# Attention scores computed twice, the second time with keys on partitions, in units of 8 heads

## The chip, the cores and the metric

The kernel runs on one core of a Trainium2 chip. Its engines are TensorE (PE, with its weight loads shown as PEld), VectorE (DVE), ScalarE (ACT), GpSimd (POOL) and SyncE (SP), which issues the DMAs. The metric is the device time of one execution in microseconds (us). Each engine works through its own queue in order; an instruction that waits holds back all that is queued behind it on that engine.

## The reference, cut to what matters

Four layers run one after the other on x of shape (4, 256, 512): attention with an adapter, a clustered feed-forward, a state-space mixer and the feed-forward again. The change lies in the first.

```python
q, k, v = split(einsum('btc,oc->bto', layernorm(x), w_attn))   # 32 heads of 16
q, k = rope(q), rope(k)
scores = einsum('bhqd,bhkd->bhqk', q, k) / sqrt(16)
attn = softmax(where(causal, scores, -inf), axis=-1)
y = einsum('bhqk,bhkd->bhqd', attn, v)
ascores = gating * softmax(einsum('bhqd,hkd->bhqk', q, ak) / sqrt(512))  # 10 adapter keys
y = y + einsum('bhqk,hkd->bhqd', ascores, av)
x = x + einsum('btc,oc->bto', y, w_proj)
```

## The kernel before

The attention stage goes through 4 batches of 256 tokens. `prepared(b)` normalises two token tiles of 128, turns them, makes queries, keys and values with three products each (operands in a high and a low part, `mm3`, L107) and applies the rotary embedding (`rotated`, L274: three DVE operations and one of POOL, L281 to L287). It is a generator: the next batch's steps are taken one by one between the units of the batch at hand.

`pieces(b, q)` (L371) takes 8 heads. `stacked` lays down high and low parts of each head as four slots of 16 (ACT L305, POOL L306), the fourth slot zero; PE turns them (tile trp, L380), and DVE copies the queries and ACT the keys out (L382). The result has 64 partitions for each head, two heads above one another, so that one product of 64 terms gives a head's scores.

A unit `u` has 4 heads, so there are 32 units. `scores(b, u)` (L413) works with queries on partitions. For each half c of the queries and each of two row positions pr (partitions 0 to 63 or 64 to 127) it fills one PSUM bank with two heads' scores over all 256 keys (L425, two products on the same 64 rows), adds the causal mask with a product of the identity and a table of -1e30 (L429), takes the row maximum on DVE (L434) and makes the exponentials on ACT, one head at a time, with the row sum as a by-product (L437). `turn` (L443) turns the exponentials on PE, 12 transposes of 128x128 for a unit (tile ptr, L452), and DVE and ACT copy them to SBUF (L453). `weigh` (L456) multiplies them with the values, four heads side by side on 32 columns each (L462 and L468), and ACT copies the product (L473). `gathered` (L476) turns it back (L479) and divides by the row sums (L484, L485).

`adapter_scores`, `adapted`, `closed` and `ended` make the adapter's part, add it, turn y (L530) and project it (tile po). In the last batch the tiles of the feed-forward that follows (tile pd, `Feed.tile`, L196) run between the units.

The main loop (L608) is a software pipeline: scores of unit i, transposes of unit i-1, weighing of unit i-2, gathering of unit i-3, then the next pieces, then one step of each waiting job. This is the order of the program text; a scheduler then reorders instructions within each engine's queue. PSUM has 8 banks: 2 for everything tagged "m", 3 for scores, 2 for transposed exponentials, 1 for the weighted values.

Of the kernel before, what the change touches and what calls it, by code (L numbers as in the profile page):

```python
# [35 lines left out]
# Columns of the constant table.  # L36
# [12 lines left out]
def constants():  # L49
    """Masks, selections and rotary tables: they depend on the shapes alone."""  # L50
# [18 lines left out]
    # [token, token tile, queries or keys, cos or sin, term]  # L69
# [8 lines left out]
def hybrid_kernel(  # L78
# [23 lines left out]
    def split(hl, v, engine=nc.vector):  # L102
        """v as the sum of two parts that each fit the products' 12 bits."""
        nc.scalar.copy(hl[0], v)  # L104
        engine.tensor_tensor(hl[1], v, hl[0].bitcast(F32), ALU.subtract)  # L105

    def mm3(o, ls, rs, first=True, last=True):  # L107
        """o = the sum over k of ls[k].T @ rs[k], operands in two parts."""
# [7 lines left out]
    def warmed(o, vs):  # L116
        """Products whose result nobody reads: they keep the array's clock up in a wait."""
        for v in vs:
            nc.tensor.matmul(o[:, : v.shape[1]], ones, v, start=True, stop=True)

    def primed(func):
        """Has the scalar engine load a function's table ahead of its use."""
# [3 lines left out]
    class Norm:  # L126
        """A layer's normalisation of x."""
# [32 lines left out]
        def turn(self, xn, tr, xs):  # L160
            """In two parts, features on partitions."""
# [4 lines left out]
        def turned(self, t, xn, tr, xs):  # L166
            """A token tile normalised, in two parts, features on partitions."""
# [4 lines left out]
    class Feed:  # L172
        """One clustered layer, a token tile at a time."""
# [22 lines left out]
        def tile(self, t, xs, halves):  # L196
            """What a token tile becomes where its columns are selected, and its hits."""
# [22 lines left out]
        def select(self, cnt, rows):  # L220
            """The columns of the clusters that any token hits, as a mask."""
# [10 lines left out]
    def attention(later):  # L232
        with ExitStack() as es:
# [6 lines left out]
            ps = pool("a_m", 2, space=PSUM)  # L240
            ps_s = pool("a_s", 3, space=PSUM)
            ps_t = pool("a_t", 2, space=PSUM)
# [31 lines left out]
            def rotated(pq, c, f, name):  # L274
                """Rotary embedding, tokens on partitions; f: 0 for queries, 1 for keys."""
# [14 lines left out]
            # Parts of 8 heads side by side so that one product of 48 terms carries  # L290
            # high * high + high * low + low * high.
            NS = 2
            stacks = [[w1.tile([P, 8, 4, HD], F32R, name=f"st{f}{i}") for i in range(NS)] for f in range(2)]
            for f in range(2):
# [6 lines left out]
            def stacked(src, f, n=P):  # L301
                st = stacks[f][turn_at[f] % NS]
                turn_at[f] += 1
# [7 lines left out]
            # Adapter keys and values, spread to block diagonals.  # L311
# [7 lines left out]
            def adapter_weights():  # L319
# [9 lines left out]
                for q in range(4):  # L329
                    s = stacked(ak[:20, q * 8 : q * 8 + 8, :], 1, 20)  # L330
# [3 lines left out]
                    # The heads' columns: two more to the right in each of the four products.  # L334
# [16 lines left out]
            vs = [w1.tile([P, 2, C + HD], F32, name=f"av{i}") for i in range(2)]  # L351
            for v in vs:
                nc.gpsimd.memset(v[:, :, C:], 0.0)
# [3 lines left out]
            def prepared(b):  # L357
                """Steps that make a batch's queries, keys and values."""
# [8 lines left out]
                for c in range(2):  # L367
                    nc.scalar.copy(vs[b % 2][:, c, :C], projected(xs[c], wv_s, where))
                    yield

            def pieces(b, q):  # L371
                """Queries and keys of 8 heads, on partitions of (2 heads, 64 terms)."""
# [29 lines left out]
            state = {}  # L402

            def begin(b):
                state[b] = {
                    "as": p2.tile([P, 2, NH, NA], F32, name="as"),
                    "rs": p2.tile([P, 2, NH], F32, name="rs"),
# [5 lines left out]
            def scores(b, u):  # L413
                """Softmax numerators of 4 heads, rows on partitions."""
                qT, kT = turned_[b, u // 2]
# [788 lines left out]
```

## Time and profile before

| what | us |
|---|---|
| median of 3 runs | 1928.0 (1927.61 to 1932.41) |
| span of the profiled execution, first to last instruction | 1929.2 |
| first score product of a batch starts at | 37.3, 122.8, 204.8, 287.0 |
| last projection of the attention ends at | 387.9 |
| granted TensorE clock, mean of the span | 0.989 |

The span lies within the range of the three runs, 1.2 us above their median. So the profiled execution can stand for them. Columns of the views: a row of a group has line, engine, operation, output and inputs, shapes and count, then the busy time in us and the mean ns of one, then the idle time of the engine before them and what ended it. A row of the time order has the start in us, the duration in us, engine and line; "x2" means that two were merged. Durations of PE's products overlap, because each starts while the one before still drains. What a product costs PE is therefore read from start to start.

### The profile page before, as it was taken

The numbers are of one execution on the slowest core, as the hardware profiler recorded it, in microseconds if no ns is written. First come the engines' busy times: TensorE is split into PE (matmuls) and PEld (weight loads), VectorE is DVE, ScalarE is ACT, GpSimd is POOL, SyncE is SP. The second block draws the span as 40 slices with busy tenths as digits, with TensorE's granted clock in tenths as the row PEclk, the third lists the DMA queues.
The fourth block names the chain that finished last, engine by engine and source line by source line (L and its number), as shares of the span: only waits on it lengthen the run. The fifth ranks groups of instructions, "written<-read, shape, count | busy, mean of one in ns | idle before, by whom it ended". The sixth has DMA issues, their size and how long they took to land.

```text
span 1929.2 us, 29952 instructions
## 1 busy us (share of the span) xinstructions
PE 1882.0 (98%) x10690; PEld 1470.6 (76%) x10690; DVE 1478.0 (77%) x2324; ACT 1383.7 (72%) x2873; POOL 346.0 (18%) x306
## 2 busy tenths in 40 slices
PE   7999999989999999999999999999999999999997
PEld 6767767767777777877787777777777777787786
DVE  5556557679998878877877797778777877877777
ACT  5665667557898677876877787778677877786753
POOL 4112120011231111122121111211111111121100
PEclk7999999989999999999999999999999999999999
DMA  4000000014555554555454455445444545455341
GB/s 140 1 1 1 1 22 24 12 38 153 166 193 182 158 166 146 154 153 164 152 164 149 154 164 160 149 144 181 148 164 151 160 157 159 133 169 158 117 126 48
DMA packets 151909, 240.35 MB, mean 125 GB/s; under 512 B 12368, under 2 KB 77520, under 8 KB 151760
## 3 DMA queue, kind: packets, MB, share of 16 engines
q1 hardware_dynamic: 151760, 238.44, 39.0%
q8 instruction: 84, 1.38, 0.3%
q14 instruction: 65, 0.53, 0.1%
HBM read 202.75 MB, written 35.65 MB: 124 GB/s over the span
## 4 chain that ended last, share of the span: by engine, by line
PE 83%; DVE 5%; ACT 5%; DMA 2%; issue 2%; SPq 0%; DVEq 0%; ACTq 0%
PE pp L112 12%; PE pp L114 12%; PE pp L113 11%; PE pyy L923 8%; PE pog L112 6%; PE pog L114 6%; PE pog L113 6%; PE sc L425 3%; PE trx L908 3%; PE ptr L452 2%; PE py L462 1%; DMA wor<-in_wout_dram 1%; PE sc L429 1%; PE trp L380 1%; DVE acc L849 1%
## 5 line engine op out<-in xcount | busy, mean ns | idle before, releaser
L112 PE MATMUL pp<-mx,w 128*128 128x512 f32 (+1 forms) x1160 | 469.1, 404 | 7.2 <-DVE acc L849 6.7
L114 PE MATMUL pp<-mx,w 128*128 128x512 f32 (+1 forms) x1160 | 459.0, 396 | 0.0
L113 PE MATMUL pp<-mx,w 128*128 128x512 f32 (+1 forms) x1160 | 458.1, 395 | 0.0
L849 DVE SCALAR_TENSOR_TENSOR acc<-pp,cw_s,acc 128x1012 f32<-128x1012 f32 (+2 forms) x240 | 304.8, 1270 | 23.7 <-ACT acc L842 23.1
L897 DVE TENSOR_TENSOR em<-em,gm 128x1536 f32<-128x1536 f32 x128 | 228.3, 1784 | 88.9 <-ACT em L891 80.6
L112 PEld LDWEIGHTS pp<-mx,w 128*128 128x128 f32 x1160 | 218.8, 189 | 68.3 <-issue 10.3
L114 PEld LDWEIGHTS pp<-mx,w 128*128 128x128 f32 x1160 | 218.6, 188 | 49.3 <-issue 0.4
L113 PEld LDWEIGHTS pp<-mx,w 128*128 128x128 f32 x1160 | 219.0, 189 | 45.1 <-issue 0.7
L946 POOL TENSOR_TENSOR sq<-sq,acc 128x1024 f32<-128x1024 f32 x55 | 132.6, 2411 | 584.0 <-ACT acc L945 584.0
L885 POOL TENSOR_SCALAR_AFFINE_SELECT r<-r 128x512 f32<-128x512 f32 x128 | 128.8, 1007 | 550.1 <-DMA r<-cumd 427.4
L104 ACT CAST w<-wr 128x512 fp32r<-128x512 f32 x144 | 88.5, 615 | 193.2 <-PE pp L113 169.9
L112 PE MATMUL pog<-wo,gh 128*128 128x512 f32 x512 | 204.2, 399 | 0.0
L114 PE MATMUL pog<-wo,gh 128*128 128x512 f32 x512 | 200.4, 392 | 0.0
L113 PE MATMUL pog<-wo,gh 128*128 128x512 f32 x512 | 199.7, 390 | 0.0
L890 ACT ACTIVATE em<-r,col_t 128x128 f32<-128x128 f32 x512 | 164.9, 390 | 48.3 <-PE pyy L923 46.9
L923 PE MATMUL pyy<-em,xd 128*64 128x256 f32 (+1 forms) x2048 | 188.7, 329 | 2.0 <-DVE em L897 1.9
L923 PEld LDWEIGHTS pyy<-em,xd 128*64 128x64 f32 x2048 | 133.1, 137 | 64.8 <-issue 21.1
L893 ACT ACTIVATE em<-r,col_t 128x128 f32<-128x128 f32 x512 | 166.4, 388 | 0.0
L881 DVE TENSOR_SCALAR em<-r,col_t 128x128 f32<-128x128 f32 x512 | 136.6, 326 | 11.8 <-PE pyy L923 10.1
L909 DVE TENSOR_TENSOR xd<-trx,dt_t 128x512 f32<-128x512 f32 x128 | 86.2, 683 | 61.6 <-PE trx L908 61.4
L105 DVE TENSOR_TENSOR w<-wr,w 128x512 fp32r<-128x512 f32 x139 | 98.0, 706 | 43.1 <-ACT w L104 42.4
L437 ACT ACTIVATE e<-sc,nmx 128x128 f32<-128x128 f32 (+1 forms) x256 | 105.4, 425 | 14.9 <-DVE nmx L434 14.8
(285 smaller groups left out, 3320.7 us busy)
## 6 DMA issues: line engine op xcount, KB each, us to landing
wr<-in_win_dram SPq DMA_DIRECT2D x287, 256.0 KB, 2.9
r<-cumd SPq DMA_DIRECT2D x128, 512.0 KB, 4.2
spill<-gb SPq DMA_DIRECT2D x63, 512.0 KB, 2.9
gr<-spill SPq DMA_DIRECT2D x120, 256.0 KB, 3.5
wor<-in_wout_dram SPq DMA_DIRECT2D x64, 256.0 KB, 3.1
out_dram<-x SPq DMA_DIRECT2D x8, 256.0 KB, 2.3
x<-in_x_dram SPq DMA_DIRECT2D x1, 1536.0 KB, 9.9
gr<-spill SPq DMA_DIRECT2D x8, 192.0 KB, 2.6
```

Source lines behind the costliest of these rows:

```text
L112: nc.tensor.matmul(o, lh, rh, start=(first and k == 0), stop=False)
L113: nc.tensor.matmul(o, lh, rl, start=False, stop=False)
L114: nc.tensor.matmul(o, ll, rh, start=False, stop=(last and k == n - 1))
L437: nc.scalar.activation(es_[c][:, 2 * j + pr, :], sc[:, j, :n], AF.Exp, bias=nm[:, j : j + 1], accum_out=rs[:, c, h : h + 1],)
L849: nc.vector.scalar_tensor_tensor(av[:, :, d:], pv[:, :, : L - d], cw_s[:, ch, tap : tap + 1], av[:, :, d:], ALU.mult, ALU.add,)
L881: nc.vector.tensor_scalar(e[:, b, 2, :], rv[:, b, 1, :], col_t[:, h, b, 1:2], 0.0, ALU.subtract, ALU.min,)
L885: nc.gpsimd.affine_select(rv[:, :, 0, :], rv[:, :, 0, :], pattern=[[0, B], [1, P]], compare_op=ALU.is_ge, fill=-1e30, base=0, channel_mult ...
L890: nc.scalar.activation(e[:, b, 1, :], rv[:, b, 1, :], AF.Exp, bias=col_t[:, h, b, 2:3])
L893: nc.scalar.activation(e[:, b, 0, :], rv[:, b, 0, :], AF.Exp, bias=col_t[:, h, b, 0:1])
L897: nc.vector.tensor_tensor(e, e, gm, ALU.mult)
L923: nc.tensor.matmul(py[d, b, k * P :], xd[:, 2 * b + k, d], es2[hh][:, b, 2 * k : 2 if k == 0 else 3, :].rearrange("p s i -> p (s i)"), sta ...
L946: (nc.gpsimd if n < NB - 1 else nc.vector).tensor_tensor(sq, sq, x2, ALU.add)
```

## The change

The transposed exponentials go. Instead the scores are computed a second time with keys on partitions, so that the exponentials come out as `weigh` needs them. The row maximum, which is now needed along the free axis of the second product, is made a term of it: slot 3 of the keys, until now zero, holds a one in its first place, and the same row of the queries receives minus the maximum. A unit is now 8 heads, so there are 16 iterations of the loop instead of 32.

For each unit, `tops` computes the first scores with the products alternating between the two row positions, masks them, takes the maxima on DVE as before (six reductions of 128x512 instead of eight of two sizes), turns the maxima on PE, copies them on ACT, and two DMAs on SP write them into the queries' rows 48 and 112. `numerators` of the unit before computes the second scores and takes the exponentials, a whole bank at a time and without a row sum; POOL then sets the entries behind the causal line to zero (`affine_select`). The row sum comes from a column of ones beside each head's 16 values. PSUM is dealt out anew: 3 banks "m", 4 for both kinds of scores, 1 for the weighted values.

```diff
-            ps = pool("a_m", 2, space=PSUM)
-            ps_s = pool("a_s", 3, space=PSUM)
-            ps_t = pool("a_t", 2, space=PSUM)
+            ps = pool("a_m", 3, space=PSUM)
+            ps_s = pool("a_s", 4, space=PSUM)
             ps_y = pool("a_y", 1, space=PSUM)
...
+            VW = HD + 1
+            vs = [w1.tile([P, 2, NH * VW + HD], F32, name=f"av{i}") for i in range(2)]
             for v in vs:
-                nc.gpsimd.memset(v[:, :, C:], 0.0)
+                nc.gpsimd.memset(v, 1.0)
+            for v in stacks[1]:
+                nc.gpsimd.memset(v[:, :, 3, 0:1].bitcast(F32), 1.0)
...
+            def tops(b, q):
+                qT, kT = turned_[b, q]
+                nm = p2.tile([P, 2, NMW], F32, name="nmx", tag="nmx")
+                def banks(parts):
+                    made = []
+                    for c, js in parts:
+                        n = (c + 1) * P
+                        pair = [
+                            ps_s.tile([P, len(js), n], F32, name="sc", tag="sc") for _ in range(2)
+                        ]
+                        for i, j in enumerate(js):
+                            for pr in range(2):
+                                rows = slice(64 * pr, 64 * pr + 64)
+                                nc.tensor.matmul(
+                                    pair[pr][:, i, :], qT[rows, j, c * P : (c + 1) * P], kT[rows, j, :n],
+                                    start=(i == 0), stop=False,
+                                )
+                        made += [(c, js, pr, sc) for pr, sc in enumerate(pair)]
+                    for c, js, pr, sc in made:
+                        n = (c + 1) * P
+                        nc.tensor.matmul(
+                            sc[:, :, n - P :], identb, negb.unsqueeze(1).to_broadcast([P, len(js), P]),
+                            start=False, stop=True,
+                        )
+                        at = pr * 4 + js[0]
+                        nc.vector.tensor_reduce(
+                            nm[:, c, at : at + len(js)], sc, AX.X, ALU.max, negate=True
+                        )
+                banks([(1, (0, 1)), (1, (2, 3))])
+                yield
+                banks([(0, (0, 1, 2, 3))])
+                tr = ps.tile([NMW, 2, P], F32, name="trm", tag="m")
+                for c in range(2):
+                    nc.tensor.transpose(tr[:, c, :], nm[:, c, :], ident)
+                mT = p2.tile([8, 2, P], F32R, name="mT", tag="mT")
+                nc.scalar.copy(mT, tr[:8])
+                for pr in range(2):
+                    load(
+                        qT[64 * pr + 48 : 64 * pr + 49].bitcast(F32),
+                        mT[4 * pr : 4 * pr + 4].rearrange("p c i -> p (c i)").bitcast(F32),
+                    )
+                yield
...
+            def numerators(b, q):
+                qT, kT = turned_.pop((b, q))
+                e = es_[b, q] = [p3.tile([P, 3, 4, P], F32, name="e", tag="e") for _ in range(2)]
+                def banks(k, js):
...
+                    for i, j in enumerate(js):
+                        for pr in range(2):
+                            rows = slice(64 * pr, 64 * pr + 64)
+                            nc.tensor.matmul(
+                                pair[pr][:, i, :], kT[rows, j, k * P : (k + 1) * P], qT[rows, j, k * P :],
+                                start=(i == 0), stop=(i == len(js) - 1),
+                            )
...
+                        nc.scalar.activation(to, sc, AF.Exp)
+                banks(0, (0, 1))
+                banks(0, (2, 3))
+                yield
+                banks(1, (0, 1, 2, 3))
+                for pr in range(2):
+                    v = e[pr][:, 0:2].rearrange("p s j i -> p (s j) i")
+                    nc.gpsimd.affine_select(
+                        v, v, pattern=[[0, 8], [1, P]],
+                        compare_op=ALU.is_ge, fill=0.0, base=0, channel_multiplier=-1,
+                    )
+                yield
...
-            def turn(es_):
...
-                    for j in range(4):
-                        nc.tensor.transpose(pt[:, j, :], src[:, j, k * P : (k + 1) * P], ident)
-                    nc.scalar.copy(dst, pt) if k else nc.vector.tensor_copy(dst, pt)
...
+                nc.vector.reciprocal(ry.unsqueeze(3), tv[:, :, :, HD : HD + 1])
...
+            for i in range(n + 3):
...
+                    top = tops(b, q)
+                num = numerators(*divmod(i - 1, 4)) if 1 <= i <= n else iter(())
+                next(top, 0)
+                next(num, 0)
+                if 0 < i < n:
+                    adapter_scores(b, q)
+                aside(1)
+                next(top, 0)
+                next(num, 0)
+                if 2 <= i <= n + 1:
+                    yss[i - 2] = weigh(*divmod(i - 2, 4))
+                aside(2)
+                if 3 <= i:
+                    bq = divmod(i - 3, 4)
+                    gathered(*bq, yss.pop(i - 3))
...
+                aside(1)
+                if i + 1 < n:
+                    pieces(*divmod(i + 1, 4))
```

`aside(k)` takes one step of each waiting job and k steps of the feed-forward's tiles. In the queues of the changed program, PE has for each unit: 8 first scores of the second query half, 4 masks, 8 second scores of the unit before, 8 first scores of the first half, 2 masks, 8 second scores, the turned maxima, then the projections and the weighing, then the transposes of the next pieces. The next batch's values are the exception: their projections stand between the scores. POOL has the two `affine_select` of a unit one after the other, with the adapter's last operation between them in each batch's last unit. SP has the two maximum DMAs of the last four units behind the feed-forward's loads and ahead of the mixer's first loads.

## Prediction

> **What bounds the kernel now.** I first cut the span at the starts of the batches' first scores (37.3, 122.8, 204.8, 287.0) and at the last projection's end (387.9), and asked for each engine's busy time there.
>
> ```profile
> 37.30:122.80 85.50, 84.83 (x535) 59.20 (x535) 45.21 (x90) 52.63 (x191) 16.60 (x26) 0.91 0.00 1
> 122.80:204.80 82.00, 81.71 (x563) 58.33 (x560) 50.09 (x106) 52.15 (x190) 14.86 (x22) 1.00 0.01 1
> 204.80:287.00 82.20, 81.44 (x563) 57.81 (x560) 50.31 (x108) 55.03 (x193) 14.98 (x23) 1.00 0.04 13
> 287.00:387.90 100.90, 97.20 (x697) 72.81 (x694) 69.54 (x176) 61.70 (x212) 6.63 (x11) 0.98 0.06 17
> ```
>
> After the length stand PE, PEld, DVE, ACT, POOL, then PE's granted clock. A batch costs 82 us; PE is never free in it, DVE and ACT are busy for 61 to 64%, POOL for 18%. So PE sets the pace, and the change can give at most what it takes off PE. The groups by shape say what that is.
>
> ```profile
> L425 PE MATMUL sc<-pc,pc 64*128 64x256 f32 x256 | 68.1, 342 | 0.4 <-ACT e L437 0.3
> L452 PE MATMUL ptr<-con,e 128*128 128x128 f32 x384 | 63.3, 279 | 0.4 <-ACT e L437 0.2 <-DVE eT L453 0.2
> L437 ACT ACTIVATE e<-sc,nmx 128x256 f32<-128x256 f32 x128 | 59.8, 479 | 11.1 <-DVE nmx L434 11.0
> L437 ACT ACTIVATION_READ_ACCUMULATOR e<-sc,nmx 128x1 f32 x256 | 52.9, 207 | 0.0
> L434 DVE TENSOR_REDUCE nmx<-sc 128x2 f32<-128x512 f32 x64 | 43.7, 686 | 20.9 <-PE sc L429 13.0 <-issue 2.5 <-ACT e L437 2.1
> L453 DVE COPY eT<-ptr 128x512 f32<-128x512 f32 x64 | 42.8, 681 | 10.8 <-PE ptr L452 10.4
> ```
>
> What a product costs PE is read in the order of time, from start to start.
>
> ```profile
> 205.47 0.50 PE L425 MATMUL sc<-pc,pc 64*128 64x256 f32 x2
> 205.90 0.28 PE L429 MATMUL sc<-negb,identb 128*128 128x256 bf16 x1
> 206.11 0.50 PE L425 MATMUL sc<-pc,pc 64*128 64x256 f32 x2
> 206.54 0.28 PE L429 MATMUL sc<-negb,identb 128*128 128x256 bf16 x1
> ...
> 226.38 0.42 PE L468 MATMUL py<-eT,av 128*32 128x128 f32 x6
> ```
>
> Two scores and a mask recur every 0.64: 0.22 from the first score to the second (same 64 rows), and 0.21 each for going to the full array and back, of which about 0.1 is the product. The last line shows six products on different column groups begun together, all over in 0.42: side by side they cost little more than one.
>
> **The change on PE, for 8 heads.** *Removed:* 8 groups of 0.64 = 5.1; 24 transposes at 0.11 (x4 takes 0.60, one 0.27) = 2.6. *Added:* 16 products of 256 columns and 16 of 128, alternating between the two row positions. No row shows two row positions at once. Ends: one after the other, 0.22 and 0.17 each (0.22 less 0.05 for half the columns), 6.2 together; or in pairs at half of that, 3.1. I take 3.2 (0.11 and 0.09), since the nearest row is the side-by-side one. Masks: 4 at 0.13 (L390, same size) and 2 at 0.23 (the 512-column products) = 1.0; turning the maxima 0.3; six changes of array shape at 0.1 = 0.6. Added 5.1, removed 7.7: PE gains **2.6 a unit, 42 us in 16 units**, if nothing waits; with products one after the other, -0.4 a unit, a small loss. The 32 weighing products and all else stay.
>
> The page "TensorE: Matmul & The Clock Gate" of the Trainium skill, part "Packing small matmuls", says that weight loads overlap running products only where the row group differs. That fits the 0.22 above and speaks for the halves; taken at its word it changes nothing in the 42.
>
> **What now waits.** The four score banks are filled three times a unit, and the queue order is fixed: scores A and B, masks, second scores, first-half scores, masks, second scores. Each step needs banks that DVE or ACT has just emptied. From t = 0 at the first score, with 0.1 per hop: 8 scores to 0.9; first mask starts at 1.0, takes 0.28; four reductions (0.686, successive ones about 0.64 apart) from 1.4 to 4.0. Second scores of pair A wait for the second reduction, 2.8 to 3.2; four exponentials of 128x512 (0.59, as ACT's copy of that shape; 0.53 apart) from 3.6 to 5.8. First-half scores when pair A is empty, 4.9 to 5.7, masks to 6.2; two reductions to 7.5; turned maxima at 7.7 to **7.9**. The last two exponentials end at 8.5. PE's own work in it is 5.2: 2.7 wait per unit eat the 2.6 that the products save. With a projection's operand copied by ACT in between it is 8.6.
>
> "TensorEngine Tiling (Array Packing)" of the Trainium skill, "PSUM Bottleneck", speaks against the change here: tiling speeds up TensorE but not PSUM evacuation. If evacuation alone paced the unit (8 rows of 0.6 to 0.7 before the last maximum, 5.5) the phase would be no shorter than that.
>
> Behind that phase comes what PE has left, from the queues:
>
> | unit of a batch | us | how |
> |---|---|---|
> | first | 18.4 | 8.6 + 12 products of 0.23 + turned y 0.5 + 12 products = 14.7; the next pieces' query copies stand on DVE behind the rotary steps (0.69+0.41+0.41) and take 2x0.68; then the adapter's scores 0.5 |
> | second | 21.3 | the same, with 2.2 of weighing and 0.7 of turned y between the projections |
> | third | 22.9 | values among the scores (9.3), 2.8 values, 0.5, weighing 1.8, 0.2, projection of y 24x0.23 = 5.6; then DVE's sum 0.69 and copies 1.4 |
> | fourth | 18.2 | 9.0; weighing waits for POOL to 12.2; then 0.6+0.5+0.5+0.5+0.9+0.5 and pieces and copies 2.5 |
> | sum | 80.8 | against 82.0 |
>
> POOL's part is the triangle. The nearest row is the mixer's:
>
> ```profile
> L885 POOL TENSOR_SCALAR_AFFINE_SELECT r<-r x128: 631/640/4677, 453.7 to 1816.0; 128x512 f32<-128x512 f32 x128
> ```
>
> Twice the size: 1.25 at the median. The mean is 1.007 (page), so 2.0; the maximum would make it 9. I take 1.25, because POOL runs beside a less loaded DVE here than there. In the fourth unit the chain is: exponentials, triangle 8.2 to 9.5, the adapter's POOL operation (1.29), second triangle to 12.1, and on PE the weighing of that unit and all behind it.
>
> *First batch:* no y to finish yet. First unit 25, as the adapter's keys (four cast, subtract and turn steps) stand ahead of the turned maxima; then 17.6 (no turned y), 15.4 (no projection of y) and 18.2 = 76.2 against 85.5. *Last batch:* no projections but tiles of 3.2 each and, in the third unit, 5.6 of y: 13.0, 18.0, 27.5, then 38 from the last unit's first score to the end of y's projection. In it: phase 9, DMA (2.4 for the smallest one of before, L708) hidden by the weighing, exponentials done at 24, triangle 27, weighing to 30, copies and turns 5, projection's rest 3. Together 96.5 against 100.9.
>
> *Costed at nothing:* ACT's lighter exponentials (6 of 0.59 for 16 of 0.48 or 0.37 and 16 read-outs of 0.21) and DVE's missing copies are off the path, PE hides them; if they did set it, the bank phase above already has them. The maximum DMAs: two of 4 KB a unit, 2.4 to 3 each. Between the turned maxima and their use lie 10 us; without that cover a unit costs 3 more. Behind them on SP stand only loads for the mixer, issued at 327 before and wanted after 395. POOL's larger fills at the start (1.0 each by the 128x1360 row of 1.24) end before it is wanted at 25.
>
> Sum: -9.3, -1.2, -1.4, -4.4 = **-16**. The span is 1929.2, so 1913; against the median of 1928.0 it would be 1912.
>
> **Rivals.** *B, the waits are covered.* If PE's queue finds work in the bank phase (late weighing products, values), the 42 stand: 1887. For it: in each third unit values do stand between the scores. Against: the other units have nothing there but a few weighing products.
>
> *C, slower: the round of the score banks is longer than 7.9.* Place: from the first score to the turned maxima, in each of 16 units. Price: if the row positions do not run side by side, scores A and B end at 1.8, so the reductions start 0.9 later; second scores add 0.45, first-half scores 0.55, the last 0.3: 2.2 a unit, 35 in all, so 1948. Or ACT and DVE have other work first in their queues, as copies of 0.6 to 0.7 each; three in a unit are as much. Point: 1.0 a unit takes my 16 away, 1.4 makes it slower by over 0.3% (5.8 us, about what a measurement here can tell from no change). A clock gated down in the waits would add to it: at 400 to 425 PE was busy for 20.5 of 25 at a granted 0.80.
>
> *D, the change does not do what it says:* the transposes go, and the time stays as the second scores cost what the transposes did and the first batch's adapter chain is worse than 25 by as much as the rest gives: 1929.
>
> **How the numbers follow.** A (forecast, 1913, own range 1898 to 1930) 0.42; B 0.18; C 0.32; D 0.08. Faster by over 0.3%: 0.30 of A and B = 0.48. Same: 0.12 of A, 0.06 of D and 0.02 of C = 0.20. Slower: the rest, 0.32. The range goes from B to C with triangles of 2.0 on top (0.75 each, some 6 us on the path of a few units): 1886 to 1955.
>
> **What would show it.** Right: batches of about 81; PE waits of 2 to 3 us in each unit, ended by DVE's maxima and ACT's exponentials; neighbouring second scores 0.11 apart; a wait of the weighing for POOL in the fourth unit. Wrong: score products 0.2 apart, triangles of 2 us and more, a clock under 1 in the batches, or batches of 72 with PE closed up.

## The result and the profile after

The changed kernel takes 1944.9 us (1940.8 to 1954.6), the kernel before, beside it on the same chip, 1928.2 (1927.6 to 1932.4): a ratio of 1.0083, 95% interval 1.0054 to 1.0113. It is slower by 17 us where 16 us less were forecast. The profiled execution has a span of 1945.3. The attention's last projection ends at 404.4 instead of 387.9, which is the whole difference.

The view by batches, cut at the first score products, with the columns of the prediction's first view (length, PE, PEld, DVE, ACT, POOL, granted clock):

```profile
36.70:120.20 83.50, 76.17 (x479) 53.28 (x478) 32.74 (x57) 33.15 (x76) 22.97 (x32) 0.81 0.00 1
120.20:206.00 85.80, 76.80 (x528) 54.07 (x528) 39.14 (x74) 34.74 (x78) 23.31 (x30) 0.88 0.01 1
206.00:297.50 91.50, 82.30 (x528) 57.47 (x528) 43.83 (x80) 39.92 (x85) 23.80 (x31) 0.83 0.06 18
297.50:404.40 106.90, 94.21 (x688) 68.47 (x688) 57.58 (x141) 45.28 (x100) 18.07 (x22) 0.90 0.04 11
```

DVE and ACT do less than before in each batch, as meant, and PE in all but the third, where it is busy for longer (82.3 against 81.4) with fewer products. From the second batch on the batches are longer all the same. The column that tells it is the granted clock: 0.91, 1.00, 1.00 and 0.98 before, 0.81 to 0.90 now.

The groups by shape and the waits of PE in the attention (the waits: who waited, for whom, us in total, times, longest):

```profile
L437 PE MATMUL sc<-pc,pc 64*128 64x256 f32 x128 | 13.1, 329 | 1.5 <-ACT pc L391 1.1
L481 PE MATMUL st<-pc,pc 64*128 64x256 f32 x128 | 24.8, 336 | 2.0 <-DVE nmx L449 1.3
L492 ACT ACTIVATE e<-st 128x512 f32<-128x512 f32 x96 | 52.5, 598 | 15.7 <-PE st L481 13.8 <-PE py L516 1.3
L449 DVE TENSOR_REDUCE nmx<-sc 128x2 f32<-128x512 f32 x64 | 39.7, 683 | 34.5 <-PE sc L444 34.5
L501 POOL TENSOR_SCALAR_AFFINE_SELECT e<-e 128x1024 f32<-128x1024 f32 x32 | 34.6, 1097 | 112.0 <-ACT e L492 111.6 <-POOL e L501 0.4
```

```profile
PE trm L458 <- DVE nmx L449: 15.1, 15, 2.5
PE try L581 <- DVE y L578: 4.6, 4, 1.8
PE sc L437 <- ACT e L492: 4.2, 7, 1.7
```

The durations are those forecast (exponentials 0.60, maxima 0.68; the triangle 1.09 where 1.25 stood). Of the 16 turnings of the maxima (trm), 15 wait for DVE, up to 2.5 us. In the order of time, the first unit of the third batch:

```profile
206.02 0.74 PE L437 MATMUL sc<-pc,pc 64*128 64x256 f32 x8 [0.28 <-ACT pc L391]
206.69 0.61 PE L444 MATMUL sc<-negb,identb 128*128 128x256 bf16 x4
...
209.92 0.66 PE L437 MATMUL sc<-pc,pc 64*128 64x128 f32 x8 [0.47 <-ACT e L492]
...
212.29 0.64 PE L458 MATMUL trm<-con,nmx 128*72 128x128 f32 x2 [0.69 <-DVE nmx L449]
...
213.85 0.63 PE L113 MATMUL pq<-wq,axs 128*128 128x512 f32 x1
...
219.16 0.39 PE L113 MATMUL pq<-wk,axs 128*128 128x512 f32 x1
```

Eight first scores take 0.67 to the start of the mask, 0.084 each: these pairs do run side by side. The eight second scores of 256 columns do so only in part, as in the fourth unit of the second batch:

```profile
186.74 1.69 PE L481 MATMUL st<-pc,pc 64*128 64x256 f32 x8 [0.32 <-DVE nmx L449]
```

Here the two products of one bank start 0.22 apart, and the next two when the next bank comes free. The round (from a unit's first score to its turned maxima) takes 6.3 in the unit above, less than the 7.7 forecast. But the projection behind it takes 0.63 per product (0.43 from start to start) instead of 0.39 (0.23). The same stretch, cut where the clock changes (columns as above):

```profile
204.73:208.15 3.42, 3.14 (x27) 2.40 (x27) 1.80 (x4) 2.40 (x7) 1.24 (x3) 1.00 0.00 0
208.15:211.56 3.41, 2.94 (x24) 1.78 (x23) 3.01 (x7) 2.56 (x5) 0.00 (x0) 1.00 0.00 0
211.56:214.97 3.41, 2.72 (x10) 1.91 (x9) 0.67 (x2) 1.45 (x3) 0.93 (x1) 0.50 0.00 1
214.97:218.39 3.42, 3.42 (x9) 2.60 (x9) 0.00 (x0) 0.00 (x0) 1.20 (x2) 0.50 0.00 1
218.39:221.80 3.41, 3.41 (x19) 2.76 (x18) 2.94 (x6) 0.00 (x0) 1.29 (x1) 1.00 0.00 0
```

After one interval of 3.4 us with gaps the clock is half for two, while PE is fully busy in the second of them.

From the starts of PE's products I split the attention (first score to the end of the last projection) into **work** (a product's time from start to start, closed up, at full clock), **clock** (what half clock adds to it) and **wait** (the rest). The stretch ends at the start of the product behind that projection, 2.2 us behind its end in e9 to e12 and at most 0.2 elsewhere. Kernels with the same products come out at 268.5 to 281.4 of work, so smaller differences of work mean little. Times are medians, and the ratios go by the kernel before as it ran beside each (medians of 1928.2 to 1930.7); e1 to e18 are the experiments below.

| kernel | time | ratio to before, 95% | attention | work | wait | clock |
|---|---|---|---|---|---|---|
| before | 1928.2 | | 350.7 | 324.7 | 16.8 | 9.2 |
| changed | 1944.9 | 1.0054 to 1.0113 | 367.8 | 268.5 | 52.3 | 47.0 |
| e1 fill | 1942.1 | 1.0049 to 1.0088 | 369.0 | 297.4 | 38.5 | 33.2 |
| e2 values | 1940.7 | 1.0038 to 1.0074 | 360.5 | 273.3 | 53.2 | 33.9 |
| e3 in turn | 1935.7 | 1.0021 to 1.0044 | 356.1 | 272.3 | 52.6 | 31.2 |
| e4 no triangle | 1921.6 | 0.9949 to 0.9980 | 350.8 | 269.2 | 49.8 | 31.7 |
| e5 mask on PE | 1935.1 | 1.0014 to 1.0054 | 349.8 | 287.7 | 49.0 | 13.1 |
| e6 spread | 1929.0 | 0.9978 to 1.0005 | 349.7 | 275.6 | 48.3 | 25.9 |
| e7 spread, mask | 1928.5 | 0.9985 to 1.0010 | 345.7 | 285.7 | 45.0 | 14.9 |
| e8 changed again | 1942.7 | 1.0057 to 1.0095 | 363.3 | 268.6 | 49.3 | 45.4 |
| e9 tail | 1936.2 | 1.0006 to 1.0040 | 348.6 | 272.4 | 51.9 | 24.3 |
| e10 tail, turn | 1929.2 | 0.9986 to 1.0011 | 341.8 | 276.9 | 48.9 | 15.9 |
| e11 tail, turn, fill | 1933.8 | 1.0009 to 1.0028 | 346.5 | 290.4 | 43.4 | 12.8 |
| e12 tail, turn, mask | 1934.5 | 1.0003 to 1.0023 | 347.0 | 284.9 | 41.0 | 21.2 |
| e13 mul on DVE | 1941.9 | 1.0037 to 1.0074 | 364.2 | 268.6 | 54.1 | 41.4 |
| e14 spread, turn | 1927.6 | 0.9972 to 1.0003 | 346.8 | 280.2 | 44.0 | 22.5 |
| e15 split triangle | 1946.0 | 1.0028 to 1.0090 | 365.0 | 270.0 | 56.7 | 38.4 |
| e16 spread, turn, mul | 1926.7 | 0.9976 to 1.0003 | 346.6 | 281.0 | 46.3 | 19.3 |
| e17 adapter later | 1926.2 | 0.9980 to 0.9999 | 345.4 | 269.4 | 47.6 | 28.4 |
| e18 all later | 1928.2 | 0.9987 to 1.0005 | 345.1 | 281.4 | 44.2 | 19.6 |

The change takes 56 us of work off PE, adds 35 of waits and 38 of clock: +17. The granted clock alone bounds the last term: the attention has 103 us at half clock against 19 before, which takes at most 52 and 9 us. The split is of one profiled execution each, the time a median of 4 to 11 runs; where the two disagree (e4, whose profiled run lay 11 us above its median), the time decides.

### The profile page after: what moved, and what is told of

Same layout as the page of the kernel before. It is cut to its first block, busy times and chain, and to the rows that moved or that the text cites. A ratio compares the mean times of both kernels' runs of the same rounds, so it can differ in the third digit from the quotient of the medians.

```text
span 1945.3 us, 29134 instructions
## 1 busy us (share of the span) xinstructions
PE 1867.0 (96%) x10562; PEld 1456.2 (75%) x10562; DVE 1437.3 (74%) x2196; ACT 1314.4 (68%) x2425; POOL 375.6 (19%) x340
## 4 chain that ended last, share of the span: by engine, by line
PE 78%; DVE 8%; ACT 7%; DMA 3%; issue 3%; POOL 2%; SPq 0%; DVEq 0%; ACTq 0%; POOLq 0%
PE pp L112 12%; PE pp L114 11%; PE pp L113 11%; PE pyy L983 8%; PE pog L112 6%; PE pog L114 6%; PE pog L113 6%; PE trx L968 3%; PE py L516 2%; DMA wor<-in_wout_dram 1%; DVE nmx L449 1%; DVE acc L909 1%; PE pq L112 1%; PE pq L114 1%; PE pq L113 1%
## 5 line engine op out<-in xcount | busy, mean ns | idle before, releaser
L909 DVE SCALAR_TENSOR_TENSOR acc<-pp,cw_s,acc 128x1012 f32<-128x1012 f32 (+2 forms) x240 | 304.9, 1270 | 23.3 <-ACT acc L902 22.6
L114 PEld LDWEIGHTS pp<-mx,w 128*128 128x128 f32 x1160 | 218.7, 189 | 49.3 <-issue 0.4
L945 POOL TENSOR_SCALAR_AFFINE_SELECT r<-r 128x512 f32<-128x512 f32 x128 | 122.4, 956 | 557.5 <-DMA r<-cumd 495.8
L950 ACT ACTIVATE em<-r,col_t 128x128 f32<-128x128 f32 x512 | 164.9, 390 | 48.9 <-PE pyy L983 47.2
L941 DVE TENSOR_SCALAR em<-r,col_t 128x128 f32<-128x128 f32 x512 | 139.2, 331 | 12.2 <-PE pyy L983 10.1
L114 PEld LDWEIGHTS pog<-wo,gh 128*128 128x128 f32 x512 | 96.1, 188 | 20.8 <-issue 0.2
```

Of the source, the lines that this page charges most:

```text
L114: nc.tensor.matmul(o, ll, rh, start=False, stop=(last and k == n - 1))
L909: nc.vector.scalar_tensor_tensor(av[:, :, d:], pv[:, :, : L - d], cw_s[:, ch, tap : tap + 1], av[:, :, d:], ALU.mult, ALU.add,)
L941: nc.vector.tensor_scalar(e[:, b, 2, :], rv[:, b, 1, :], col_t[:, h, b, 1:2], 0.0, ALU.subtract, ALU.min,)
L945: nc.gpsimd.affine_select(rv[:, :, 0, :], rv[:, :, 0, :], pattern=[[0, B], [1, P]], compare_op=ALU.is_ge, fill=-1e30, base=0, channel_mult ...
L950: nc.scalar.activation(e[:, b, 1, :], rv[:, b, 1, :], AF.Exp, bias=col_t[:, h, b, 2:3])
```

## The experiments

**e1: filling in the waits.** `fill(o, n)` issues n products of 128x256 that nobody reads.

```diff
+                tr = ps.tile([P, 4, P], F32, name="trm", tag="m")
+                fill(tr[:, 2:4, :], 4)
                 banks([(0, (0, 1, 2, 3))])
-                tr = ps.tile([NMW, 2, P], F32, name="trm", tag="m")
+                fill(tr[:, 2:4, :], 8)
+                tr = tr[:NMW]
...
```

> The changed kernel with 12 products more in each unit of 8 heads, whose results nobody reads: 4 of 256 columns ahead of the first-half scores, 8 ahead of the turned maxima. They need nothing and run on PE while it would wait there (0.47 us and 0.69 us in the trace of the changed kernel). Theory 'clock': the waits of the bank round are about as long as forecast, but PE's clock is halved behind them (99 us of the attention at a granted 0.5, against 19 before), and that is what made the change a loss. Then the filling keeps the clock up; the waits stay, filled; the time falls by most of the 39 us which the halved clock adds, less up to 0.3 us a unit for filling beyond the wait: 1905 to 1925. Rival 'round': the waits themselves are the loss and the halved clock falls into time that is lost anyway; then the filling gains nothing and costs 0 to 5 us: 1943 to 1952.

Measured: 1942.1, three us less, which the spread of the changed kernel's runs (1940.8 to 1954.6) holds: far from the range of "clock", and 1 us under that of "round". The first units of the second and third batch, first in the changed kernel, then filled:

```profile
120.20:140.40 20.20, 19.05 (x126) 13.53 (x126) 10.31 (x19) 7.46 (x19) 6.76 (x9) 0.83 0.00 1
206.00:225.90 19.90, 18.72 (x124) 13.34 (x124) 10.31 (x19) 7.43 (x18) 6.67 (x9) 0.83 0.01 1
```

```profile
122.60:140.50 17.90, 17.65 (x139) 12.68 (x138) 10.33 (x19) 7.92 (x18) 6.40 (x8) 1.00 0.01 1
207.00:224.90 17.90, 17.61 (x136) 12.64 (x136) 10.32 (x19) 7.59 (x18) 6.72 (x9) 1.00 0.01 1
```

With twelve products more the unit is 2.0 to 2.3 shorter, with the clock at 1.00: against "round", the clock costs time of its own. But in all, 14 less of wait and 14 less of clock stand against 29 more of work. In the fourth units the clock still fell (for 10.2 us from 193.2 and from 275.1).

**e2: values of the next batch in the first units' rounds.** A pause of one step ahead of the values in `prepared`, which starts one step earlier.

> The changed kernel with the next batch's projections dealt out anew: the step that normalises the first token tile runs one step earlier, at the end of the batch before, and a pause of one step comes ahead of the values. So in the first three units of each batch 12 products of 512 columns, for queries or values, stand in PE's queue inside the bank round, where the first two units had nothing but waits. No work is added or left out. Theory 'clock': six more rounds have their wait (about 2.3 us) covered and their gated stretch (about 2.4 us) gone: about 1917, 1910 to 1928. Rival 'round' (only the waits cost): 6 x 2.3 = 14 less, 1931. If the DVE steps of the rotary embedding, which now come between the maxima, delay these by as much, nothing is gained: 1945.

Measured: 1940.7, 4 us less and not the 28 that "clock" expected, nor the 14 of "round". By the split the clock term is 13 less, the waits as they were.

**e3: the score products in turn.** `for pr in range(2)` stands outside `for i, j in enumerate(js)` in `tops` and `numerators`.

> The changed kernel with both kinds of scores in another order: first all products of one row position, then all of the other, instead of alternating. This asks for the term of 3.2 us a unit (row positions side by side). The trace of the changed kernel has 8 products of 256 columns in 0.67 us, 0.084 each, against 0.22 for products on the same rows before. Taken in turn they should cost 0.2 each again, so PE's work rises by about 3 us a unit. Theory 'round': the scores lie on the path of the round and the time rises by about 2.2 a unit, 35 in all, to 1980. Theory 'clock': part of the added work lies in waits and keeps PE's clock up, so the rise is smaller: 1950 to 1970. If the order does not matter, 1945.

Measured: 1935.7, nine less; all three expectations missed. Eight products still take 0.677 against 0.671. But their starts come in pairs in both traces (at 0.00, 0.01, 0.22 and 0.23 us in e3), so it isn't shown that PE's queue held one row position behind the other at all, and what the order costs stays open. With about the same work and waits, only the clock is 16 less. The scheduler had put other things in another order with the edit, which e13 and e17 go into.

**e4: without the triangle** (`affine_select` left out).

> The changed kernel without POOL's triangle: the exponentials behind the causal line are not set to zero, so that the weighing takes in keys that come after the query. This takes away the wait of the weighing for POOL, 6.5 us in all by the releasers of the changed kernel's trace, most of it in the fourth units. Both theories: 1938 to 1945, the clock's windows move a little. Rival 'triangle': POOL's chain in the fourth units is the loss, then 16 us or more go: below 1930.

Measured: 1921.6, 23 less, by its number the rival. But PE's queue changed too (in the fourth units more of the weighing stands ahead of the adapter's transposes), and e13 and e15, which change POOL's queue, gave little or nothing by their medians. So it is not shown to be POOL's time. What goes with it is the clock: the median granted clock of e4's runs is 0.984, that of the changed kernel's eight (with e8) 0.970, which is some 31 against some 59 us of lost clock in the whole kernel.

**e5: the triangle as a product on PE.** The second scores get the mask, POOL's step goes:

```diff
-                                start=(i == 0), stop=(i == len(js) - 1),
+                                start=(i == 0), stop=False,
...
+                        nc.tensor.matmul(
+                            sc[:, :, :P], identb, negbt.unsqueeze(1).to_broadcast([P, len(js), P]),
+                            start=False, stop=True,
+                        )
...
```

> The changed kernel with POOL's triangle replaced by a product: the second scores get -1e30 behind the causal line from the identity times a turned table, as the first scores do (per unit four products of 256 columns and two of 512, by the rows of the changed kernel's trace 4 x 0.11 + 2 x 0.23 = 0.9 us of PE). Nothing is left out. Leaving the triangle away altogether gave 1921.6. Theory 'POOL' (the weighing is late because of the triangle): 1921.6 plus at most 16 x 0.9, so 1922 to 1936. Theory 'clock': the same, but the products run inside the bank round, where PE waits, and keep its clock up: 1915 to 1925. If the gain without the triangle came from something else than PE's wait for POOL: 1940 and more.

Measured: 1935.1, 13.5 more than e4: the mask costs nearly its 14 us. That lies at the upper end of "POOL" (1922 to 1936), and "clock" missed. Yet the ten runs, which differ by 19 us, show the clock's price at its plainest: 1924.9 us at a mean clock of 0.992, 1943.8 at 0.980, the others between. Lost clock is 0.008 x 1924.9 = 15 and 0.020 x 1943.8 = 39 us: 24 more for 19 us of time, over the whole kernel.

**e6: the side work spread.** Queries in the rounds of the first two units, values in the third and fourth, the adapter's part one step later, its halves in the next batch's first unit (the last batch as it was).

> The changed kernel, triangle on POOL as it was, with the side work dealt out anew: queries of the next batch in the rounds of the first two units, values in those of the third and the fourth, and the adapter's part one step later, so that its sums no longer stand on DVE between the maxima of the fourth unit, and its two halves come in the first unit of the next batch. The last batch is left as it was. No work is added or left out. Putting projections into the rounds of the first two units alone gave 1940.7. Theory 'fourth unit' (the loss left after that is in the fourth units, which took 21 to 24 us where 18.2 were forecast, with DVE's adapter sums ahead of the last maxima and PE at half clock behind it): 3 x 3 to 4 us less, 1928 to 1933. Rival (the loss is POOL's triangle and the last batch): 1938 to 1942.

Measured: 1929.0: "fourth unit" as expected, level with the kernel before. **e7** adds the mask of e5:

> Both together: the side work dealt out anew and the triangle as a product on PE. If the round's waits, the halved clock behind them and POOL's triangle are three separate losses, their cures add up: the gain of the mask (see the run of it alone) and that of the dealing out, together 1908 to 1920, faster than the kernel before. If they are one and the same idle time, cured once: as the better of the two alone.

Measured: 1928.5, as the better of the two alone. The cures don't add up: 10 more work, 3 less wait, 11 less clock.

**e8: the changed kernel again.**

> The changed kernel once more, beside these, to see how far its time moves between chips and runs: 1940 to 1950. The halved stretches of PE's clock should lie elsewhere than in the first profile, as they start at fixed intervals of 3.4 us whose phase differs from run to run; their sum in the attention, 99 us, should come within 20 of that.

Measured: 1942.7; halved for 102 us in the attention against 103 in the first profile by the split's count (the 99 expected goes by product starts).

**e9 to e12: the tail.** The feed-forward's tiles are held back in the last three iterations until y is turned, and y's projection takes the last step of its sums, for both token tiles, behind all others; e10 takes the products in turn besides; e11 adds six fillings a unit to that, e12 the mask of e5 instead.

> The kernel with the side work dealt out anew (1929.0), and besides the end of the attention mended: the last tiles of the feed-forward that stood ahead of the last unit's second scores are held back until its products of y are to be turned, where PE waited 1.8 and 1.7 us for DVE. No work is added or left out. Theory 'tail' (the last unit took 46 to 52 us instead of the 38 forecast, because its second scores stood behind a tile of 3.2 us and its end has bare waits): 5 to 8 us less, 1921 to 1924, and the attention ends with fewer tiles left. Rival: PE does the same products anyway, the tiles only move, and PE's clock is halved in the last unit instead, which loses it a cover: 1927 to 1931.

> The same with the score products of one row position after the other, which took 9 us off the changed kernel while the eight products of 256 columns took as long (0.677 against 0.671 us). If the order really shortens the round: 4 to 9 us less than the run before this in the list. If the 9 us came from how the rounds happened to fall on the 3.4 us intervals of the clock: no difference beyond 3 us.

> The same once more with 6 products of 256 columns, read by nobody, ahead of the turned maxima, where PE still waits 0.7 to 1.0 us in most units: 0.65 us of filling in a wait that is there anyway. Theory 'clock': of the halved stretches left in the attention (57 us in the run with the side work dealt out anew, 26 us of time lost by them) half or more go, and the filling costs little: 8 us or more less than the run before this in the list. Rival 'round': no gain, 0 to 5 us more for delaying the second scores of the second half.

> The run with the tail mended and one row position after the other, with the triangle as a product on PE instead of POOL's: 0.9 us more of PE a unit, no wait for POOL. Dealing out alone and dealing out with the mask gave the same time (1929.0, 1928.5) with 55 and 30 us of halved clock. So no difference beyond 4 us from the run without the mask; if the clock is what the mask bought, it should be the better the fewer waits are filled otherwise, so here 0 to 5 us worse than the filled run.

Measured: 1936.2, 1929.2, 1933.8, 1934.5. The attention ended earlier (383.6 in e9 and 376.1 in e10, 385.3 in e6), but the tiles then stood behind it: the mixer's first product starts at 411.1 in e9 and at 404.7 in e10, at 405.4 in e6. So the rival of e9 holds, and was still too low. Products in turn were worth 7 again, in the range of "the order shortens the round"; but three of e9's ten runs took 1928 to 1929, as long as e10, and e14 doesn't bear it out. Filling cost 4.6: the clock term fell by 3, work rose by 14. "Clock", in the form that filling pays, is refuted. The mask cost 5, a little over the 4 expected at most, and 1 more than filling, as the second half of the expectation has it.

**e13: the adapter's multiplication off POOL; e15: the triangle in two halves.**

```diff
-                nc.gpsimd.tensor_tensor(sc, sc, wide(sa), ALU.mult)
+                nc.vector.tensor_tensor(sc, sc, wide(sa), ALU.mult)
```

> The changed kernel with one instruction moved: the adapter's last multiplication (once a batch, 128x640) on DVE instead of POOL, where it stood between the two triangles of the fourth unit. Nothing is left out. Theory 'POOL queue' (taking the score products in turn gained 9 us only because the order of POOL's queue came out differently in the fourth units, both triangles ahead of the multiplication, so that the weighing no longer waits for it): the fourth units fall from 21 to 24 us to about 20, the time to 1933 to 1938. Rival (the order of the score products itself shortens the rounds): no gain here, 1940 to 1948.

> The changed kernel with each of POOL's triangles cut in two of 128x512: the first half as soon as the first half's exponentials are there, the second behind it. POOL's work stays or grows a little (four of 0.63 for two of 1.09), but the last one the weighing waits for is half as long, and it no longer stands behind the adapter's multiplication alone. Theory 'POOL queue': between the changed kernel and the one without a triangle (1921.6): 1928 to 1938. Rival (the gain without the triangle came from less traffic or from the clock, not from the weighing's wait): 1940 to 1948.

Measured: 1941.9 and 1946.0, both in the rivals' ranges. By the medians "POOL queue" falls: neither POOL's order nor the length of its last step made e3 faster. It falls less clearly than that sounds, as two of e15's five runs took 1933 and 1935 and two of e13's six 1936 and 1937, under any of the changed kernel's. Nor is the order of the products, e13's rival, shown by it. The fourth unit of the second batch in e13, then in e3 (PE's queue):

```profile
187.67 0.64 PE L458 MATMUL trm<-con,nmx 128*72 128x128 f32 x2 [2.48 <-DVE nmx L449]
188.25 1.06 PE L516 MATMUL py<-e,av 128*32 128x256 f32 x2
189.82 1.08 PE L560 MATMUL pt<-con,as 128*80 128x128 f32 x4 [0.52 <-DVE as L554]
```

```profile
189.28 0.64 PE L458 MATMUL trm<-con,nmx 128*72 128x128 f32 x2 [2.45 <-DVE nmx L449]
189.85 2.34 PE L516 MATMUL py<-e,av 128*32 128x256 f32 x18
192.13 1.08 PE L560 MATMUL pt<-con,as 128*80 128x128 f32 x4
```

The wait for the maxima is the same. In e3, 18 weighing products follow it closed up, ahead of the adapter's transposes (pt); in e13 two, and then the next wait. The clock is half for 6.8 us there in e3, for 10.2 in the changed kernel.

**e14 and e16: spread and in turn,** e16 with e13's edit too.

> The side work dealt out anew (1929.0) and the score products in turn, without the mended tail, which moved tiles behind the attention and gained nothing. If the two are separate gains: 1920 to 1924, faster than the kernel before. If both cure the fourth unit, once: 1927 to 1930.

> The side work dealt out anew, the score products in turn, and the adapter's multiplication on DVE. With the dealing out the adapter's part has left the bank round of the fourth unit already, so POOL's queue should have nothing to give: within 3 us of the run without the multiplication on DVE; if it gives 4 us more, the POOL queue still held the weighing.

Measured: 1927.6 and 1926.7; cured once, not twice, and nothing more from POOL's queue.

**e17: the adapter one step later,** nothing else.

```diff
-                    if q == 3:
-                        jobs.append(adapted(b))
                     top = tops(b, q)
...
                     yss[i - 2] = weigh(*divmod(i - 2, 4))
+                if i < n and i % 4 == 3:
+                    jobs.append(adapted(i // 4))
                 aside(2)
```

> The changed kernel with one thing moved: the adapter's part begins one step later in each batch's fourth unit, so that its two sums no longer stand on DVE between the maxima (where the turned maxima waited 2.5 us) and some of the weighing stands ahead of the adapter's transposes on PE, as in the run with the products in turn. Projections stay where they were. Theory 'fourth unit': the wait there falls to 0.7 us as in the other units and the clock is back one or two intervals earlier; the four fourth units give 3 to 4 us each: 1930 to 1935. Rival (the first two units' rounds carry the loss, and the dealing out gained by these): 1940 to 1946.

Measured: 1926.2, 19 less than the changed kernel from one step moved: more than expected. DVE in the fourth unit of the second batch, changed kernel and e17:

```profile
185.99 2.48 DVE L449 TENSOR_REDUCE nmx<-sc 128x2 f32<-128x512 f32 x4 [1.19 <-PE sc L444]
188.40 0.81 DVE L547 TENSOR_REDUCE anm<-as 128x64 f32<-128x640 f32 x1
189.61 0.69 DVE L449 TENSOR_REDUCE nmx<-sc 128x4 f32<-128x512 f32 x1 [0.41 <-PE sc L444]
191.37 0.82 DVE L551 TENSOR_REDUCE asum<-as 128x64 f32<-128x640 f32 x1 [1.07 <-ACT as L549]
192.11 0.68 DVE L449 TENSOR_REDUCE nmx<-sc 128x4 f32<-128x512 f32 x1
```

```profile
180.78 0.81 DVE L547 TENSOR_REDUCE anm<-as 128x64 f32<-128x640 f32 x1
182.27 1.29 DVE L449 TENSOR_REDUCE nmx<-sc 128x4 f32<-128x512 f32 x2 [0.69 <-PE sc L444]
183.75 0.82 DVE L551 TENSOR_REDUCE asum<-as 128x64 f32<-128x640 f32 x1 [0.19 <-ACT as L549]
```

In the changed kernel the adapter's sum (L551) stands between the last two maxima and itself waits 1.07 for a chain over POOL and ACT; the last maximum is held back though its scores are long there. In e17 it stands behind both. The turned maxima on PE, with that wait in the changed kernel and without it in e17:

```profile
192.84 0.64 PE L458 MATMUL trm<-con,nmx 128*72 128x128 f32 x2 [2.47 <-DVE nmx L449]
183.62 0.64 PE L458 MATMUL trm<-con,nmx 128*72 128x128 f32 x2
```

In the profiles the fourth units of the first three batches take 18.0, 18.0 and 18.7 us instead of 21.7, 21.0 and 24.1: 12 of the 22 us by which the attention is shorter. What is left isn't tied to the edit, as other units of the changed kernel differ by up to 3 us between its two profiles, the first and e8 (23.2 and 20.3 for the second unit of the third batch). By the split 19 of the 22 are clock and 5 wait. But the clock does not come back early in each of these units: in the second batch it is half for 10.2 us in e17 too (181.4 to 191.7), in the third for 6.8 instead of 13.7. The batches of e17:

```profile
36.90:114.20 77.30, 69.20 (x465) 47.76 (x464) 32.14 (x56) 32.34 (x74) 23.35 (x33) 0.88 0.00 1
114.20:195.40 81.20, 74.33 (x530) 51.71 (x530) 38.98 (x74) 34.67 (x78) 23.32 (x31) 0.92 0.01 2
195.40:275.90 80.50, 72.14 (x530) 51.14 (x530) 43.70 (x80) 39.76 (x85) 23.81 (x32) 0.96 0.07 21
275.90:382.20 106.30, 96.88 (x701) 72.76 (x702) 57.59 (x142) 45.63 (x101) 17.80 (x22) 0.89 0.04 11
```

77.3, 81.2 and 80.5 are, within 1.1 us, the 76.2 and 80.8 of the prediction. That is luck in part: 28 us of half clock, which the prediction did not have, stand in e17's attention against more work saved than the 42 forecast. The last batch is 10 over its 96.5.

**e18: the same in e16's last batch.**

> The version with side work dealt out anew, products in turn and the adapter's multiplication on DVE (1926.7), with the adapter's part one step later in the last batch too, which had been left as it was. Theory 'fourth unit': 3 to 4 us less, 1922 to 1924, faster than the kernel before by over 0.3%. Rival (in the last batch the adapter's part then ends later and the closing waits for it): 1927 to 1931.

Measured: 1928.2: the rival's range. No version beats the kernel before by over 0.3%; e17 at 0.9990 (0.9980 to 0.9999) comes nearest, but for e4, which leaves work out.

## Why the prediction was wrong, step by step

The step that failed is the cost of the half clock: the sum had no term for it. It stood in rival C only, without a price ("would add to it"), and among the signs of being wrong as "a clock under 1 in the batches", which is what came. By the split it is 38 us, more than the 32 between the forecast and the time. Work and waits alone come to -56 + 35 = -21, close to the forecast -16, but by two errors that cancel in part: each was off as said below.

- *PE's work:* forecast -42, by the split -56. The first scores ran side by side as taken (0.084 and 0.075 against 0.11 and 0.09), so "no row shows two row positions at once" is answered. The second scores of 256 columns mostly did not: of 92 that directly follow another, the median starts 0.22 behind it, where 0.11 was named as the sign of being right, as their banks come free one by one. So the 14 us must come from elsewhere in the main; the runs don't separate from where.
- *The waits:* -42 and the sum of -16 leave 26 us of waits; measured +35. The round is shorter than drawn (6.3 in the first unit shown, 7.8 in a fourth, against 7.7 and 9.0), the exponentials and maxima as long as drawn. So rival C's place, a round longer than 7.9, is wrong though its sign is right.
- *The first three units of a batch:* 18.4, 21.3, 22.9 forecast; in e17 20.3 and 18.7, 20.2 and 20.3, 22.6 and 22.8 (second and third batch). In the changed kernel 20.2 and 19.9, 21.7 and 23.2, 22.9 and 24.2. (The terms written out for the first and the third add up to 18.1 and 22.3, short of the sums beside them. And ACT's share of the third batch before is 67%, not within 61 to 64%; the argument doesn't change.)
- *The fourth unit:* 18.2 forecast, 21.0 and 24.1 measured. The weighing was not held until 12.2; it began at 8.4. But the wait of 2.5 for the maxima behind the adapter's sum was not seen, and the clock was half for 10.2 us behind it. e17 takes that wait away (0.5 is left in the third batch): 18.0 and 18.7. How much of its 19 us is the wait and how much the weighing ahead of the transposes isn't separated; e3, with the second alone, had 9.
- *The last unit:* 38 forecast, 45.8 measured, 47.6 in e17. All 24 products of y's projection come at its end (5.9 us, 3 forecast), and its second scores stand behind a tile. Not mended (e9).
- *Costed at nothing:* the DMAs of the maxima, rightly (no wait in the profile is put down to them); that ACT's and DVE's lighter work gains nothing of itself, not tested.
- *The skill's rules:* "PSUM Bottleneck" of "TensorEngine Tiling (Array Packing)" holds in kind: of PE's waits, 15.1 us stand ahead of the turned maxima, until DVE has read the score banks, and 5.5 ahead of scores that need a bank which ACT or DVE empties (4.2 and 1.3). The rest of the 35 isn't put down to banks. The rule that mattered was not weighed: "TensorE: Matmul & The Clock Gate" of the Trainium skill, "A second HAM failure mode: psum-queue depth-cycling", says that short idle times of PE between groups, as banks are cycled, make the clock swing. The trace agrees, with waits of 0.3 to 0.7 us in the first unit shown, up to 2.5 in the fourth units, and halvings of 3.4 to 13.7.

What stays open: why no cure that leaves nothing out goes below 1926. The waits stay at some 40 to 57 us in every run without filling, and work put into them costs about what it covers. Which part of the clock's loss hangs on which wait isn't shown either: e17 shortens one wait a batch, and the clock still falls.

## What to carry to other kernels

Work taken off an engine that was closed up can turn into gaps unless the steps around it get shorter too, and on PE the gaps had a second price here, half clock for 3.4 to 13.7 us at a time in the changed kernel: price both in the sum. Look for the instruction that a foreign chain puts between two steps of the critical round, as the adapter's sum here; moving it gained 19 us here, filling 3 at best. And compare the queues of all engines before an experiment's result is put down to its edit.

## What the runs showed of the hardware

PE's clock fell to half without an idle time of 3.4 us: the longest single one in the attention of the 20 profiles is 3.0 us (e15), in the changed kernel 2.5. I cut these attentions at the 3.4 us steps of the clock and took PE's busy share, as the views have it, of each interval at full clock. Of 160 intervals under 0.7, 102 were followed by half clock; of 175 between 0.7 and 0.8, 41; of 229 between 0.8 and 0.9, 22 (the one shown above, 2.94 of 3.41, is among them); of 1153 above 0.9, 7. The page named above, in "Part 1: The HAM clock gate", has the clock halve after at least one idle interval of that length; here intervals over half full did it, so the measurement decides. The kernel before shows the same once, at the end of its attention, where PE waits for DVE:

```profile
376.91:380.33 3.42, 1.43 (x8) 0.82 (x8) 2.62 (x7) 1.02 (x3) 0.00 (x0) 1.00 0.00 0
380.33:383.74 3.41, 3.35 (x9) 2.80 (x10) 0.42 (x1) 1.66 (x2) 0.00 (x0) 0.50 0.03 5
```

Its other full-clock intervals there are 0.79 full or more, and it kept its clock.
